# A Mamba-2, MLP and mixture-of-experts layer on one core: first transposes in two banks, statistics pinned behind a VectorE step, the output norm's chain ranked ahead, and the first MLP started a piece later

## The chip, the cores and the metric

The kernel runs on one core of a Trainium2 chip. The metric is the time on the device in microseconds (us) of one execution. Several executions are taken and their median is given. One further execution is recorded by the hardware profiler; the profile is of that one.

## The reference

The input is a sequence of 2048 tokens with 512 features, all in float32. The layer has two parts, each with a residual. The first part is a layer norm followed by an RMS norm, a Mamba-2 block, and an MLP with a gate. The second part is a layer norm and a mixture of experts with eight experts of which two are chosen for a token.

```
x = x + attn_part(layernorm(x))
x = x + moe(layernorm(x))

attn_part(v):  h = v + mamba2(rmsnorm(v, ln1_w));  h2 = rmsnorm(h, ln2_w)
               return h + silu(h2 @ gate_w) * (h2 @ up_w) @ down_w

mamba2(u):     z, xb, B, C, dt = split(u @ in_proj_w)
               xb, B, C = silu(causal_conv4(xb, B, C));  dt = softplus(dt + dt_bias)
               y = ssd_chunked(xb * dt, dt * A, B, C)        # chunks of 128 tokens, a state carried
               y = rmsnorm((y + D * xb) * silu(z), norm_w)
               return y @ out_proj_w
```

The state-space step works on chunks of 128 tokens: inside a chunk it is a masked product, and between chunks a state of 16 heads is carried on.

## The kernel before

**Tiling.** The 2048 tokens are 16 tiles of 128 tokens (index `t`) and 8 blocks of 256 tokens (index `b`, two tiles each, `j` = 0 or 1). The features lie on the partitions in four pieces of 128 (`NK` = 4). The MLP works on blocks of 512 tokens (index `fb`, four of them), which is two Mamba blocks.

**A block of the Mamba part.** `prepare(b)` (L201) takes the row statistics of the block's two tiles (`scales`, L182: bn_stats and bn_aggr on VectorE, a square root on ScalarE, a reciprocal), makes the normalised rows `hn` (L211), and turns each into columns with four TensorE transposes and one weighted copy from PSUM by VectorE (`transposed`, L189, its copy at L197). The result is `hT`. It then makes the step sizes: the product `pdt` (L228), softplus by arithmetic and an exponential, `dA` (L259), the cumulated sum `pc` (L262), and small products (L272 to L288). The rows go to memory (L267, L268) and are read back spread over the partitions by `spread` (L291: two loads of `cum` at L298 with a mask on GpSimd, and four loads of `ec` at L310 for every tile but the first). `project` (L332) makes one pair of projection columns in PSUM (`pm`, L326, weights `wi`), copies them (L338), runs the convolution on VectorE (L345, L347) and silu on ScalarE (L353). There are six such pairs, and four `gate` pairs (L355, product `pz`).

**A chunk.** `chunk(b, j, ...)` (L381) is a generator whose steps are interleaved by hand with the above. For each half of the heads (`gp`) it makes scores `psc` (L400), exponentials on ScalarE (L406), their products on VectorE (L408), for the first half the weighted inputs `xd` (L414, one buffer that is shared with `sq`), then the products `py` (L423 from the state, L431 inside the chunk) and the state's update (L438 to L459). Then the squares of y are taken on ScalarE and added on GpSimd (`sq`, L467 to L470; the last addition is kept as `summed`), the output projection `po` (L475) and the sum of squares `pms` (L478) run, and the output norm follows (L480 to L492): root and reciprocal `ry`, the new rows `h` (L484), their addition to the residual on GpSimd, a store from ScalarE's queue, a second square and root, and the scaling of `h`. The last step of a chunk turns `h` into `h2T` (L498). It is left over and run in the next chunk as `ninth`.

**PSUM.** `ps_tr` has one bank, "tr", which all transposes and the small products share. `ps_mm` has two banks, "mm", also called kind "d". `ps_y` has one bank, for `py` and `po`.

**Order of the work.** The Tile planner orders each engine's instructions by walking a model of the time: at each moment it issues the ready instruction that was traced first. Loads without an open dependency, such as those of the MLP's weights, are issued long ahead of where they are written. `tc.high_priority(n)` ranks an instruction as if traced n instructions earlier. `tc.issue_after(ins)` puts those instructions of a block that run on the engine of `ins` behind `ins` in that engine's queue; it does not make them wait for its end. From block 2 on (`BPF` = 2) TensorE's order is no longer planned: `manual_schedule` (L887) keeps it as traced. The tracing order is made by `mamba(b)` (L810), which yields 32 times in a block, and by the loop at L881, which at such a yield runs `advance()`: one piece (a quarter of one of 16 column steps) of the MLP of the 512 tokens that are done. The MLP's weights come in as `mg` (L513 to L515) and `ms` (L526); in the first MLP GpSimd makes sums and differences of them (L516, L517, L527, L528), which ScalarE's queue stores for the later ones (L529, L530).

The condition for `advance()` in the code before is

```
            if b > BPF or b == BPF and n > 1:
                advance()
```

After the last block the remaining pieces run, and after two of them the last `ninth`. The last MLP then overlaps the routing, and the experts follow.

Of the kernel before, what the change touches and what calls it, by code (L numbers as in the profile page):

```python
# [15 lines left out]
P = 128  # L16
# [33 lines left out]
def mamba_mlp_moe(ctx, tc, x, w_in, w_out, w_gu, w_down, par, wr, wg, wu, wd, out):  # L50
# [93 lines left out]
        nc.vector.bn_stats(out=st, in_=src)  # L144
        nc.vector.bn_aggr(out=dst, in_=st)

    AT_ONCE = 400

    early = const.tile([P, 1], F32, name="early")
    nc.scalar.activation(early, eps, AF.Sqrt)  # L150
# [22 lines left out]
        pool, tag = use[kind]  # L173
        return pool.tile([P, *shape], F32, name=name, tag=tag)

    idle = ps_y.tile([P, P], F32, name="idle", tag="y")
    for _ in range(20):
        nc.tensor.transpose(idle, ident, ident)

# [6 lines left out]
        nc.scalar.activation(rboth[:, lo:hi], mv[:, lo:hi, 1], AF.Sqrt, bias=eps2, scale=1.0 + EPS)  # L186
        nc.vector.reciprocal(rboth[:, lo:hi], rboth[:, lo:hi])

    def transposed(src, dst, weight=None):  # L189

        pt = bank("tr", [NK, P], "pt")
        for k in range(NK):
            nc.tensor.transpose(pt[:, k, :], src[:, k * P : (k + 1) * P], ident)  # L193
        if weight is None:
            nc.scalar.copy(dst, pt)  # L195
        else:
            nc.vector.tensor_tensor(dst, pt, bc(weight, 2, P), ALU.mult)  # L197

    first_rows = None

    def prepare(b):  # L201

        nonlocal first_rows
        hT = wa.tile([P, NK, TB], F32, name=f"hT{b}", tag="hT")
        hns = []
        with tc.issue_after(first_rows) if b == 1 else ExitStack():
            scales(b)
            for j in range(NCH):
                t = b * NCH + j
                hns.append(wa.tile([P, D], F32, name=f"hn{t}", tag="tok", bufs=3))  # L210
                normed = nc.vector.tensor_scalar(  # L211
                    hns[j], res[t], mv[:, t, 0:1], rboth[:, t : t + 1], ALU.subtract, ALU.mult
                )
        if b == 0:
            first_rows = normed.ins
        for j in range(NCH):
            yield
            transposed(hns[j], hT[:, :, j * P : (j + 1) * P], params[:, C_L1 : C_L1 + NK])

        yield hT  # L220
        lo, hi = b * NCH, (b + 1) * NCH
# [158 lines left out]

    def chunk(b, j, dt, ncum, dtdec, cd, cum, ec, xb, cs, zs):  # L381

        nonlocal summed
# [7 lines left out]
        for gp in range(2):  # L391

            if t:
                with tc.issue_after(summed):
                    nc.gpsimd.tensor_tensor(ec[:, gp], ec[:, gp], cs[gp][:, :, tok], ALU.mult)

            psc = ps_sg.tile([P, 2, 4, P], F32, name=f"psc{t}_{gp}", tag="sg")
            for half in range(2):
                rows = halves[half]
                nc.tensor.matmul(psc[:, half], xb[rows, 2 + gp, tok], cs[gp][rows, :, tok], start=True, stop=True)  # L400


            lt = cum[gp].rearrange("p (a i) q -> p a i q", a=2)
            turns = [(half, i, 8 * gp + 4 * half + i) for i in range(4) for half in range(2)]
            for half, i, h in turns:
                nc.scalar.activation(lt[:, half, i], lt[:, half, i], AF.Exp, bias=ncum[:, j, h : h + 1])  # L406
            for half, i, h in turns:
                nc.vector.scalar_tensor_tensor(  # L408
                    lt[:, half, i], lt[:, half, i], dt[:, j, h : h + 1], psc[:, half, i], ALU.mult, ALU.mult
                )  # L410
            if gp == 0 and t < NT - 1:

                xd = wa.tile([P, 4, 4, HD], F32, name=f"xd{t}", tag="xd", bufs=1)
                nc.vector.tensor_tensor(  # L414
                    xd, bc(xbt[:, 0], 2, 4),
                    bc(dtdec[:, j, :].rearrange("p (g i) -> p g i", g=4), 3, HD), ALU.mult,
                )
            if gp:
                yield
            py = ps_y.tile([P, 4, P], F32, name=f"py{t}_{gp}", tag="y")  # L420
            if t:
                for i in range(4):
                    nc.tensor.matmul(  # L423
                        py[:, i, :], sdt[:, gp, i, :], ec[:, gp, i, :], start=(i == 0), stop=False,
                        skip_group_check=True,
                    )
# [53 lines left out]
        ry = wa.tile([P, 1], F32, name=f"ry{t}", tag="ry")  # L480
        rsqrt_eps(ry, pms, scale=1.0 / DI)
        h = wa.tile([P, D], F32, name=f"h{t}", tag="tok", bufs=3)
        nc.vector.tensor_scalar(h, res[t], mv[:, t, 0:1], rstd[:, t : t + 1], ALU.subtract, ALU.mult)
        nc.vector.scalar_tensor_tensor(h, po, ry, h, ALU.mult, ALU.add)  # L484
        nc.gpsimd.tensor_tensor(res[t], res[t], h, ALU.add)
        nc.scalar.dma_start(out=resd[t], in_=res[t])

        m2 = wa.tile([P, 1], F32, name=f"m2{t}", tag="m2")
        nc.scalar.activation(sq[:, 4:8, :].rearrange("p a q -> p (a q)"), h, AF.Square, accum_out=m2)
        r2 = wa.tile([P, 1], F32, name=f"r2{t}", tag="r2")  # L490
        rsqrt_eps(r2, m2, scale=1.0 / D)
        nc.vector.tensor_scalar_mul(h, h, r2)  # L492
        yield
        fb, off = divmod(t * P, FB)
        if off == 0:
# [314 lines left out]
    def mamba(b):  # L810
# [12 lines left out]
        for j in range(NCH):  # L823
            pieces = chunk(b, j, dt, ncum, dtdec, cd, *near[j], xb, cs, zs)
            for _ in range(4):
# [55 lines left out]
    for b in range(NB):  # L881
# [296 lines left out]
```

## Time and profile before

| what | value |
|---|---|
| median of 3 runs | 1582.25 us (1581.88 to 1583.77) |
| profiled execution, its own time | 1582.87 us |
| its span, first to last instruction | 1580.9 us |
| TensorE's mean granted clock | 0.990 |
| busy: TensorE, VectorE, ScalarE, GpSimd | 1537.3, 776.9, 753.2, 404.2 us |
| memory moved | 218.68 MB, mean 138 GB/s |

In a profile PE is TensorE's matmuls, PEld its weight loads, DVE VectorE, ACT ScalarE, POOL GpSimd and SP the engine that issues most loads. A line of the timeline has the start in us, the time until the group's end in us, the engine, the line of the kernel, the operation, output and inputs with their shapes, the number of instructions, and in brackets the idle time ahead of it with what ended that. A float32 matmul appears as two records. A line of the stretches has the stretch, its length, the busy time with the number of instructions that began in it, then the granted clock, the share of the memory engines and GB/s.

### The profile page before, as it was taken

The numbers are of one execution on the slowest core, as the hardware profiler recorded it, in microseconds if no ns is written. First come the engines' busy times: TensorE is split into PE (matmuls) and PEld (weight loads), VectorE is DVE, ScalarE is ACT, GpSimd is POOL, SyncE is SP. The second block draws the span as 40 slices with busy tenths as digits, with TensorE's granted clock in tenths as the row PEclk, the third lists the DMA queues.
The fourth block names the chain that finished last, engine by engine and source line by source line (L and its number), as shares of the span: only waits on it lengthen the run. The fifth ranks groups of instructions, "written<-read, shape, count | busy, mean of one in ns | idle before, by whom it ended". The sixth has DMA issues, their size and how long they took to land. (4 is left out here: it accounts for less than half of the span.)

```text
span 1580.9 us, 19196 instructions
## 1 busy us (share of the span) xinstructions
PE 1537.3 (97%) x6303; PEld 1052.7 (67%) x6303; DVE 776.9 (49%) x2018; ACT 753.2 (48%) x1346; POOL 404.2 (26%) x510
## 2 busy tenths in 40 slices
PE   7899979999999999999999999999999999999997
PEld 6666666767666677767676777666777666555553
DVE  6776755754556464646555554434454352222221
ACT  3888796745663778457748543222211221111110
POOL 3442324333341212121212112011111123333331
PEclk8999989999999999999999999999999999999999
DMA  8443435544554553333344533238777233333332
GB/s 287 143 154 115 140 117 177 181 151 153 177 198 142 167 164 116 128 127 129 128 163 151 167 95 101 89 95 298 239 239 237 83 62 60 63 64 67 67 67 33
DMA packets 127456, 218.68 MB, mean 138 GB/s; under 512 B 11584, under 2 KB 71488, under 8 KB 127360
## 3 DMA queue, kind: packets, MB, share of 16 engines
q1 hardware_dynamic: 105088, 166.08, 33.1%
q0 software_dynamic: 8736, 20.45, 7.3%
q10 hardware_dynamic: 13536, 30.94, 5.1%
q8 instruction: 52, 0.85, 0.2%
q14 instruction: 44, 0.36, 0.1%
HBM read 176.01 MB, written 41.42 MB: 138 GB/s over the span
## 5 line engine op out<-in xcount | busy, mean ns | idle before, releaser
L685 PE MATMUL pd<-md,a 128*128 128x512 f32 x512 | 238.4, 592 | 0.0
L326 PE MATMUL pm<-hT,wi 128*128 128x256 f32 x768 | 188.9, 392 | 2.3 <-DMA wi<-in_w_in 2.3
L326 PEld LDWEIGHTS pm<-hT,wi 128*128 128x128 f32 x768 | 144.6, 195 | 27.9 <-issue 6.9
L686 DVE TENSOR_TENSOR r<-r,pd 128x512 f32<-128x512 f32 x128 | 87.6, 684 | 139.7 <-PE pd L685 139.0
L685 PEld LDWEIGHTS pd<-md,a 128*128 128x128 f32 x512 | 97.0, 190 | 74.1 <-issue 66.2
L347 DVE SCALAR_TENSOR_TENSOR ca<-pre,params,ca 128x256 f32<-128x256 f32 x288 | 135.0, 528 | 0.2
L701 PE MATMUL py<-h2T,ms 128*128 128x256 f32 x512 | 131.6, 379 | 1.6 <-POOL ms L527 0.8
L326 PE MATMUL pz<-hT,wi 128*128 128x256 f32 x512 | 118.9, 385 | 0.0
L1034 PE MATMUL epg<-ew,xgT 128*128 x312 | 118.1, 460 | 0.4 <-issue 0.2
L766 POOL TENSOR_TENSOR a<-a,up 128x256 f32<-128x256 f32 x64 | 47.3, 739 | 277.5 <-DVE up L760 240.4
L1034 PE MATMUL epu<-ew,xgT 128*128 x312 | 117.8, 459 | 0.0
L475 PE MATMUL po<-w_o,zs 128*128 128x512 f32 x256 | 112.8, 594 | 0.0
L406 ACT ACT_TABLE_LOAD x76 | 97.5, 1283 | 27.7 <-DVE ncum L274 19.2
L1055 PE MATMUL epd<-ew,ehT 128*128 (+1 forms) x234 | 107.1, 593 | 1.0 <-DVE ehT L1048 1.0
L701 PEld LDWEIGHTS py<-h2T,ms 128*128 128x128 f32 x512 | 95.6, 190 | 17.3 <-ACT up L740 1.6
L326 PEld LDWEIGHTS pz<-hT,wi 128*128 128x128 f32 x512 | 96.1, 193 | 15.6 <-issue 1.9
L406 ACT ACTIVATE cum<-cum,ncum 128x128 f32<-128x128 f32 x256 | 86.3, 393 | 7.9 <-POOL cum L300 4.3
L475 PEld LDWEIGHTS po<-w_o,zs 128*128 128x128 f32 x256 | 48.2, 190 | 57.0 <-issue 55.7
L1015 POOL DMA_INDIRECT xg<-xnd,idx x39 | 38.9, 997 | 175.9 <-PE pt L193 173.8
L1034 PEld LDWEIGHTS epu<-ew,xgT 128*128 128x128 f32 x312 | 59.3, 190 | 33.0
L1061 POOL DMA_INDIRECT out<-ey,idx x39 | 61.9, 1588 | 66.8 <-DVE ey L1060 40.8
L195 ACT COPY xgT<-pt 128x512 f32<-128x512 f32 x39 | 22.8, 587 | 117.7 <-PE pt L193 117.7
(248 smaller groups left out, 2567.7 us busy)
## 6 DMA issues: line engine op xcount, KB each, us to landing
wi<-in_w_in SPq DMA_DIRECT2D x80, 512.0 KB, 3.8
ms<-late SPq DMA_DIRECT2D x48, 512.0 KB, 3.6
mg<-early SPq DMA_DIRECT2D x48, 384.0 KB, 3.7
md<-in_w_down SPq DMA_DIRECT2D x64, 256.0 KB, 3.8
cum<-rowsd SPq DMA_DIRECT2D x32, 512.0 KB, 4.0
late<-ms ACTq DMA_DIRECT2D x16, 512.0 KB, 2.7
ec<-rowsd SPq DMA_DIRECT2D x60, 128.0 KB, 3.7
xnd<-xn ACTq DMA_DIRECT2D x28, 256.0 KB, 3.8
```

The source lines that it names most:

```text
L326: nc.tensor.matmul(pm[:, m, :], w[:, k, m * P : (m + 1) * P], hT[:, k, :], start=(k == 0), stop=(k == NK - 1))
L347: nc.vector.scalar_tensor_tensor(ca, pre[:, m, k : k + TB], cw[:, k : k + 1], ca, ALU.mult, ALU.add)
L406: nc.scalar.activation(lt[:, half, i], lt[:, half, i], AF.Exp, bias=ncum[:, j, h : h + 1])
L475: nc.tensor.matmul(po, y[:, m, :], w_o[:, m, :], start=(m == 0), stop=(m == 7))
L685: nc.tensor.matmul(pd, a[:, j * P : (j + 1) * P], d, start=(m == 0), stop=(m == 1))
L686: nc.vector.tensor_tensor(rows[j], rows[j], pd, ALU.add)
L701: nc.tensor.matmul(ps, w[:, k], m[:, k], start=(first and k == 0), stop=(k == KH - 1), skip_group_check=True)
L766: nc.gpsimd.tensor_tensor(a[:, 1], a[:, 1], up, ALU.mult)
L1015: nc.gpsimd.indirect_dma_start(out=xg, out_offset=None, in_=src, in_offset=bass.IndirectOffsetOnAxis(ap=idx[:, n : n + 1], axis=0))
L1034: nc.tensor.matmul(ps, xT[:, k, :], w[:, lo : lo + EI], start=(k == 0), stop=(k == NK - 1))
L1055: nc.tensor.matmul(pd, hT[:n, m, :], w[:n, NG + m * D : NG + (m + 1) * D], start=(m == 0), stop=(m == len(ET) - 1))
L1061: nc.gpsimd.indirect_dma_start(out=out, out_offset=bass.IndirectOffsetOnAxis(ap=idx[:, n : n + 1], axis=0), in_=y, in_offset=None, compute ...
```

## The change

1. `transposed` takes the kind of bank. In `prepare(0)` the second tile's transposes use a bank of kind "d" instead of "tr". Five more idle transposes follow them (`idling(5)`).
2. The statistics and normalised rows of every block but the first are put behind a VectorE instruction: those of block 1 behind the copy of block 0's last transposes, those of a later block b+1 behind `xd` of tile 2b. Before, only block 1 was held, behind block 0's last `hn`.
3. The output norm (L480 to L492) is traced under `tc.high_priority(100)`.
4. The GpSimd sums of the first MLP's early weights are put behind the newest `summed`.
5. In the first stage `spread` of tile 1 is traced after all six pairs instead of after the third.
6. In `mamba` the leftover `ninth` comes one yield later, after the step of `halves` instead of ahead of it, and the first MLP's first piece one yield later (`n > 2`).

```diff
-    AT_ONCE = 400
+    AT_ONCE, SOON = 400, 100
...
-    idle = ps_y.tile([P, P], F32, name="idle", tag="y")
-    for _ in range(20):
-        nc.tensor.transpose(idle, ident, ident)
+    def idling(n):
+        idle = ps_y.tile([P, P], F32, name="idle", tag="y")
+        for _ in range(n):
+            nc.tensor.transpose(idle, ident, ident)
+
+    idling(20)
...
-    def transposed(src, dst, weight=None):
-
-        pt = bank("tr", [NK, P], "pt")
+    def transposed(src, dst, weight=None, kind="tr"):
+
+        pt = bank(kind, [NK, P], "pt")
...
-            nc.vector.tensor_tensor(dst, pt, bc(weight, 2, P), ALU.mult)
-
-    first_rows = None
+            return nc.vector.tensor_tensor(dst, pt, bc(weight, 2, P), ALU.mult).ins
+
+    behind = None
...
-        with tc.issue_after(first_rows) if b == 1 else ExitStack():
+        with tc.issue_after(behind) if b else ExitStack():
             scales(b)
...
-        if b == 0:
-            first_rows = normed.ins
         for j in range(NCH):
             yield
-            transposed(hns[j], hT[:, :, j * P : (j + 1) * P], params[:, C_L1 : C_L1 + NK])
+            kind = "d" if b == 0 and j else "tr"
+            turned = transposed(hns[j], hT[:, :, j * P : (j + 1) * P], params[:, C_L1 : C_L1 + NK], kind)
+            if b == 0:
+                behind = turned
+                if j:
+                    idling(5)
...
-                nc.vector.tensor_tensor(
+                added = nc.vector.tensor_tensor(
                     xd, bc(xbt[:, 0], 2, 4),
...
+                if t:
+                    behind = added.ins
...
+        with tc.high_priority(SOON):
+            ry = wa.tile([P, 1], F32, name=f"ry{t}", tag="ry")
+            rsqrt_eps(ry, pms, scale=1.0 / DI)
...
+            nc.vector.tensor_scalar_mul(h, h, r2)
         yield
...
-            nc.gpsimd.tensor_tensor(w[:, 1], w[:, 3], w[:, 1], ALU.add)
-            nc.gpsimd.tensor_tensor(w[:, 2], w[:, 1], w[:, 0], ALU.subtract)
+            with tc.issue_after(summed):
+                nc.gpsimd.tensor_tensor(w[:, 1], w[:, 3], w[:, 1], ALU.add)
+                nc.gpsimd.tensor_tensor(w[:, 2], w[:, 1], w[:, 0], ALU.subtract)
...
-            near = [spread(0, j, ready[-1]) for j in range(NCH)]
+            near = [spread(0, 0, ready[-1])]
             nc.sync.dma_start(out=w_o, in_=w_out.rearrange("(t p) n -> p t n", p=P))
+    near.append(spread(0, 1, ready[-1]))
...
                 next(pieces)
+                next(halves, None)
+                yield
                 if n % 4 == 0:
                     finish(ninth)
-                next(halves, None)
-                yield
...
-            if b > BPF or b == BPF and n > 1:
+            if b > BPF or b == BPF and n > 2:
                 advance()
```

More of the change, by code (lines that the diff above doesn't have):

```diff
@@ L196, in transposed @@
         else:
-            nc.vector.tensor_tensor(dst, pt, bc(weight, 2, P), ALU.mult)
-    first_rows = None
+            return nc.vector.tensor_tensor(dst, pt, bc(weight, 2, P), ALU.mult).ins
+    behind = None
     def prepare(b):
-        nonlocal first_rows
+        nonlocal behind
         hT = wa.tile([P, NK, TB], F32, name=f"hT{b}", tag="hT")
         hns = []
-        with tc.issue_after(first_rows) if b == 1 else ExitStack():
+        with tc.issue_after(behind) if b else ExitStack():
             scales(b)
@@ L210, in prepare @@
                 hns.append(wa.tile([P, D], F32, name=f"hn{t}", tag="tok", bufs=3))
-                normed = nc.vector.tensor_scalar(
+                nc.vector.tensor_scalar(
                     hns[j], res[t], mv[:, t, 0:1], rboth[:, t : t + 1], ALU.subtract, ALU.mult
                 )
-        if b == 0:
-            first_rows = normed.ins
         for j in range(NCH):
             yield
-            transposed(hns[j], hT[:, :, j * P : (j + 1) * P], params[:, C_L1 : C_L1 + NK])
+            kind = "d" if b == 0 and j else "tr"
[4 more added lines that the diff above has]
+                    idling(5)
         yield hT
@@ L381, in chunk @@
     def chunk(b, j, dt, ncum, dtdec, cd, cum, ec, xb, cs, zs):
-        nonlocal summed
+        nonlocal summed, behind
         t = b * NCH + j
@@ L478, in chunk @@
         nc.tensor.matmul(pms, sq[:, 0, :], ones[:, 0:1], start=True, stop=True)
[L480 to L492, printed above, removed]
+        with tc.high_priority(SOON):
+            ry = wa.tile([P, 1], F32, name=f"ry{t}", tag="ry")
+            rsqrt_eps(ry, pms, scale=1.0 / DI)
+            h = wa.tile([P, D], F32, name=f"h{t}", tag="tok", bufs=3)
+            nc.vector.tensor_scalar(h, res[t], mv[:, t, 0:1], rstd[:, t : t + 1], ALU.subtract, ALU.mult)
+            nc.vector.scalar_tensor_tensor(h, po, ry, h, ALU.mult, ALU.add)
+            nc.gpsimd.tensor_tensor(res[t], res[t], h, ALU.add)
+            nc.scalar.dma_start(out=resd[t], in_=res[t])
+            m2 = wa.tile([P, 1], F32, name=f"m2{t}", tag="m2")
+            nc.scalar.activation(sq[:, 4:8, :].rearrange("p a q -> p (a q)"), h, AF.Square, accum_out=m2)
+            r2 = wa.tile([P, 1], F32, name=f"r2{t}", tag="r2")
+            rsqrt_eps(r2, m2, scale=1.0 / D)
+            nc.vector.tensor_scalar_mul(h, h, r2)
         yield
```

## The prediction

> **What bounds the kernel now.** I read the page's busy table and slices first, then TensorE's own waits, then the clock by stretches, then the timeline of the places that these named.
>
> ```profile
> PE 1537.3 (97%) x6303; PEld 1052.7 (67%) x6303; DVE 776.9 (49%) x2018; ACT 753.2 (48%) x1346; POOL 404.2 (26%) x510
> ...
> PE   7899979999999999999999999999999999999997
> ```
>
> TensorE (PE) is busy for 97% of the span. Only 1580.9 - 1537.3 = 43.6 us are idle, and the slices under 9 lie in the first 240 us and at the end. From 300 to 1500 us the stretches add to about 5.4 us of idle. A change that takes no matmul away can therefore win only in the first 240 us. TensorE's waits, longest first (total, times, longest):
>
> ```profile
> PE pt L193 <- DVE mv L145: 7.1, 1, 7.1
> PE py L423 <- POOL halo L340: 4.0, 2, 2.4
> PE pc L262 <- POOL pre L339: 3.4, 1, 3.4
> PE pm L326 <- DMA wi<-in_w_in: 2.3, 1, 2.3
> PE pt L193 <- DVE hT L197: 1.9, 1, 1.9
> ```
>
> The releaser is the last by semaphore, not always the cause. The POOL copies at L339 and L340 take 0.2 us and gate nothing here: pc waits for dA (L259, done at 27.81 us), and py waits for h (L484) to empty the one bank of ps_y.
>
> Idle time also slows what follows. Stretches, with TensorE's busy time, then its granted clock:
>
> ```profile
> 27.00:29.10 2.10, 1.15 (x6) 1.00 1.03 399
> 29.10:32.50 3.40, 3.40 (x10) 0.50 0.71 211
> 32.50:36.00 3.50, 3.50 (x20) 0.99 0.91 233
> ...
> 46.10:49.50 3.40, 3.40 (x10) 0.51 0.55 202
> ...
> 203.20:213.50 10.30, 4.47 (x13) 0.50 0.22 70
> ```
>
> [...] The timeline has the places:
>
> ```profile
> 8.88 1.12 PE L193 MATMUL pt<-ident,hn 128*128 128x128 f32 x4 [1.87 <-DVE hT L197]
> 10.78 3.60 PE L228 MATMUL pdt<-w_dt,hT 128*128 128x16 f32 x16 [0.78 <-DVE hT L197]
> 14.21 10.32 PE L326 MATMUL pm<-hT,wi 128*128 128x256 f32 x36
> 20.28 0.69 DVE L144 BATCH_NORM_STATS2 bn<-x 128x6 f32<-128x512 f32 x1 [3.46 <-DMA x<-in_x]
> 27.95 0.38 PE L262 MATMUL pc<-tri,dA 128*32 128x128 f32 x2 [3.42 <-POOL pre L339]
> 45.49 5.41 PE L326 MATMUL pm<-hT,wi 128*128 128x256 f32 x16 [2.35 <-DMA wi<-in_w_in]
> 206.63 1.21 DVE L414 TENSOR_TENSOR xd<-xbt,dtdec 128x1024 f32<-128x1024 f32 x1
> 209.03 1.08 PE L193 MATMUL pt<-ident,h 128*128 128x128 f32 x4 [7.07 <-DVE mv L145]
> 209.91 5.37 PE L326 MATMUL pz<-hT,wi 128*128 128x256 f32 x16
> ```
>
> The DVE line shows the statistics of tile 4, which belong to block 2, in the middle of block 0's softplus: VectorE stands 3.46 us for a load that nobody needs yet, and dA comes late.
>
> [...]
>
> **Part by part.**
>
> *Start, 6 to 61 us.* The second transposes go to a "mm" bank, so the 1.87 us wait goes. The statistics of blocks 1 and 2 leave the front of VectorE, so hT is copied at about 7.1 and 7.8 us instead of 8.15 and 10.03, and the 0.78 us before pdt goes too. pdt would run from 7.9 us. With few gaps the clock should hold. Matmuls at full clock: 16 pdt take 1.85 us (67.22 us) and 16 pm take 3.62 us (74.06 us), so half clock cost 1.75 us on pdt, 10.32 - 36 x 0.226 = 2.2 us on pm, and 0.5 us on pt. dA comes without the 3.46 us stall: the 3.42 us wait and about 1.6 us of slow clock after it go. The broadcast loads of chunk 1 (L298, L310) no longer stand before wi of pair 5 on SP's queue; they stood there until 40.25 us, waiting for rowsd. The 2.35 us wait and 1.8 us of slow clock go. TensorE's side sums to 1.87 + 0.78 + 0.5 + 1.75 + 2.2 + 3.42 + 1.6 + 2.35 + 1.8 = 16.3 us.
>
> Two things come late next. The loads: wi of pairs 0 and 1 landed a median 7.1 us after issue, so at about 10.7 us, 0.8 us after pdt; wi of pair 3 is issued at 14.5 us or later and stands behind w_o (landed 19.6 us), x and the MLP's ms (22.1 us), at 400 GB/s, so it lands at 22 to 23.5 us, against 21.7 us when three pairs are done. I charge 2 us: 14 us are left. Then VectorE: a pair's convolution is 2 x (0.31 + 3 x 0.48) = 3.5 us, six pairs 21 us, and the first starts after pm 0, at 15.0 instead of 20.98 us: 6.0 us. About 3.5 us of its later idle was waiting for TensorE (0.44 at 30.43 us, 1.15 at 29.80, 2 of the 3.0 before 52.01) and goes. So py at 61.17 us can move by about 9.5 us, and TensorE's other 4.5 us turn into a wait for VectorE there, as the four gates (14.5 us) do not cover more. ScalarE did 34.7 us up to 63 us and also allows it; its 4.41 us idle before 25.25 us, behind the ACT-queue writes of the MLP's weights, goes since those now come at 195 us. I take **-9.5**; bounds -3 (loads late, ScalarE full) and -15.
>
> *Five idle transposes*: 5 x 0.15 = 0.8 us at most, beside a wait for hn of 0.63 us: **+0.2** (0 to +0.5).
>
> *Output norm in front* (L480 to L492). Its rank moves ahead of the 100 instructions traced before it. What delayed ry at 123 and 199 us and r at 206.43 us on ScalarE was mostly exp and silu traced after it, taken since ready; rank does not change that. The waits of py are 2.4 and 1.5 us. **-0.5** (0 to -3).
>
> *Block 2's beginning, 202 to 219 us.* Before, TensorE stood 7.07 us for h, then ran 0.5 + 1.75 us slow. Now one gate (16 pz, 3.62 us) comes ahead of the transposes, from 202 to 205.6 us, and the MLP starts a piece later. But the next item in TensorE's fixed order is the transposes of hn, and hn's statistics now queue on VectorE behind xd, which ended at 207.84 us. From there: 2 x 0.67 + 2 x 0.17 = 1.7 us, a table load and root on ScalarE 1.28 + 0.29 with up to 1 us of queue, reciprocal 0.15, hn 0.54: 212 to 213 us. Then pt 0.6, gate 3.62 with up to 1.75 of slow clock, pt 0.6: the MLP's first product at 217.3 to 219.4 us, against 219.01 + 0.6 with the same work done. **-1.2** (+2 to -8, the last if xd and the statistics come ahead of the convolution).
>
> *The same order in blocks 1 to 6.* The transposes of h (L498) and of hn (L218) now stand back to back in the one bank "tr"; a gate lay between them before. The second set waits for the copy of the first: 0.69 us at L197 (347.93 + 0.60, copy 348.57 to 349.26). In block 2 this lies under the wait for hn, in block 1 the planner can part them. Blocks 3 to 6: 4 x 0.8 = **+3.2**. Bounds: the copy began 0.03 to 0.2 us after the transposes at these places, but up to 2.9 us after at others (98.70 us). In these blocks hn itself is in time: xd ended at 339.2 us, the transposes ran at 354.41 us, 15 us later against a chain of 5.
>
> *POOL's sums of the first MLP's weights* (L516, L517), each 0.8 to 0.9 us, go from 21 to 27 us to after sums of chunk 3 at 194.7 us. Behind them stand POOL's ec, state and a. POOL is idle 196 to 200 and 202 to 208 us: **0**. Cover gone, each costs its 0.9 us; one wait of this kind is there now (0.80 us at 255.16 us).
>
> *The last piece* of the MLP after the last block: moved, not added. 0.
>
> Sum: -9.5 + 0.2 - 0.5 - 1.2 + 3.2 = **-7.8 us**. The profiled execution took 1582.87 us, 2.0 more than its span and 0.6 over the median of 1582.25. Against the median: **1574.5 us**.
>
> **Rivals.** *Gate cover works whole*: hn is ready by 207 us, so block 2 gains 8 us instead of 1.2, and the start gains 11 or 12: 1582.3 - (11.5 + 0.5 + 8 - 3.2 - 0.2) = 1565.7 us. For it: TensorE asks only 3.62 + 0.6 + 0.8 us of cover. Against: xd waits for the square of h (202.57 us) and stood behind the convolution and L408. *The start is taken by loads and ScalarE*: the memory engines moved 400 GB/s from 10 to 19 us, ScalarE is 89% busy from 60 to 80 us; the start gains 3: 1581 us. Against: the MLP's 1.3 MB of early writes leave this stretch. *Slower: the copy in bank "tr" is late*. Place: L197 between L498 and L218 in blocks 2 to 6. Price 5 x (delay + 0.75). It outweighs the 11 us of gains from a delay of 1.5 us on; at 2.9 us it is 18.3 us: 1589.5 us. For it: such delays are in the trace where VectorE was in a convolution. Against: at these places it answered within 0.2 us.
>
> **How the numbers follow.** Within 0.2% (3.2 us) a measurement cannot tell from no change. The forecast, 1569 to 1579 us, 0.50; whole cover 0.20; start taken 0.19; slower 0.11. The start-taken case is split 0.10, 0.07, 0.02 over faster, the same and slower. Faster 0.50 + 0.20 + 0.10 = 0.80, same 0.07, slower 0.02 + 0.11 = 0.13. The range leaves out the worst of the slower case and the far end of the best one: 1561.5 to 1582.5 us.
>
> **What would show it.** Right: pt at 7 to 8 us without a wait, no statistics with a DMA wait on VectorE, pc and pair 5's pm without waits, py of chunk 0 at about 51.5 us; a new wait of pt for h2T (L197) of about 0.8 us in four or five blocks; hn's wait at block 2. Wrong: long new TensorE waits at 25 to 60 us for wi or silu; L197 copies over 1 us late; TensorE waiting for POOL's sums in the first MLP.

## The result and the profile after

The changed kernel takes 1597.16 us (median of 6 runs, 1594.77 to 1598.65) against 1582.9 us (median of 6 runs of the kernel before beside it, 1580.96 to 1584.23). The ratio is 1.0088, with a 95% interval of 1.0075 to 1.0101: it is **slower by 0.9%**, 14.3 us. The forecast was 7.8 us faster, and its range ended at 1582.5 us. The profiled execution took 1597.42 us, its span is 1595.7 us, and TensorE's mean granted clock 0.989.

The first view is the page's busy table and slices of the changed kernel.

```profile
PE 1543.7 (97%) x6308; PEld 1051.4 (66%) x6308; DVE 770.5 (48%) x2018; ACT 741.4 (46%) x1335; POOL 399.9 (25%) x510
...
PE   9999888999999999999999999999999999999997
```

The early slices are fuller than before: the start did gain. The idle time is 1595.7 - 1543.7 = 52.0 us, 8.4 more than before, and busy time rose by 6.4 us with five instructions more. From the first product of the MLP to the experts TensorE is idle for 21.0 us, against 5.6 before, in waits that are too short to show in slices of 40 us; ahead of that stretch it is idle for 7 us less than before. TensorE's own waits show them (total, times, longest, in us):

```profile
PE px L711 <- DVE a L775: 9.9, 7, 1.8
PE py L431 <- POOL halo L346: 7.5, 2, 5.0
PE pt L196 <- DVE hn L214: 4.8, 2, 3.7
PE pt L196 <- DVE h2T L200: 3.1, 4, 0.8
```

(Lines have moved: transposes are L196, their copy L200, the MLP's product L711, the weight stores L539 and L540.) The first line was forecast nowhere: the MLP's products wait for their own bank (0.5 us, once, before the change). The fourth is the one that the forecast named, 4 x 0.78 us.

**Where the time went.** I marked the start of each tile's output projection (`po`, L483; L475 before), of the first MLP product (`px`), and of the experts in both traces. Changed minus before:

| mark | after - before, us |
|---|---|
| `po` of tile 0 | -9.95 |
| `po` of tile 3 | -9.0 |
| first `px` (MLP starts) | -4.4 |
| `po` of tile 4 | -4.3 |
| `po` of tile 6 | +2.1 |
| `po` of tile 8 | +4.3 |
| `po` of tile 12 | +9.7 |
| experts start | +14.8 |

Marks with a sign are such differences below too; before the change `po` of tile 0 starts at 78.93 us. So there are two stories. The start gains 10 us, as forecast (9.5). Then 4.6 us go at block 2's beginning, between `po` of tile 3 and the first `px`, and 19.2 us while MLP pieces and blocks share the engines. The experts add nothing.

**Block 2's beginning.** The timeline of the changed kernel, GpSimd, ScalarE with its queue (ACTq), and TensorE:

```profile
189.99 1.40 POOL L527 TENSOR_TENSOR mg<-mg 128x256 f32<-128x256 f32 x2
190.74 0.33 ACTq L539 DMA_DIRECT2D early<-mg  x1
192.10 0.33 ACTq L540 DMA_DIRECT2D late<-ms  x1
192.45 1.28 ACT L139 ACT_TABLE_LOAD   x1 [3.16 <-POOL pre L345]
195.21 2.05 PE L431 MATMUL py<-ec,sdiag 128*128 128x128 f32 x8 [4.98 <-POOL halo L346]
203.27 0.63 PE L196 MATMUL pt<-ident,h 128*128 128x128 f32 x4 [1.51 <-DVE mv L145]
207.63 1.09 PE L196 MATMUL pt<-ident,hn 128*128 128x128 f32 x4 [3.73 <-DVE hn L214]
```

Read from the top: the pinned sums run on GpSimd until 191.4 us and the difference made of them (L538) until 192.1; ScalarE's queue holds the two stores of these, and only behind them stands the table load for `ry`. ScalarE stood 3.16 us. The releaser that the line names, a copy at L345, gates nothing; e3 below shows that it is the sums. So `ry`, `h` and with it `py`'s bank come late: `py` waits 4.98 us (1.53 before). The wait of `pt` for h fell from 7.07 to 1.51 us, but one for hn of 3.73 us follows. The clock was 0.50 from 192.4 to 199.2 and from 206.1 to 212.9 us, 13.6 us in all against 10.2 us before.

**The border of two column steps.** The next view is the timeline at one of the seven places where `px` waits:

```profile
267.51 1.88 PE L695 MATMUL pd<-md,a 128*128 128x512 f32 x4
267.70 0.29 ACT L139 ACTIVATE r<-m,singles 128x1 f32<-128x1 f32 x1
268.01 1.28 ACT L739 ACT_TABLE_LOAD   x1
269.30 0.42 ACT L739 ACTIVATE a<-a 128x256 f32<-128x256 f32 x1
269.43 0.69 DVE L696 TENSOR_TENSOR r<-r,pd 128x512 f32<-128x512 f32 x1 [1.72 <-PE pd L695]
270.30 0.49 DVE L501 TENSOR_SCALAR h<-h,r 128x512 f32<-128x512 f32 x1
270.70 0.41 DVE L775 TENSOR_TENSOR a<-a,px 128x256 f32<-128x256 f32 x1
271.17 1.13 PE L711 MATMUL px<-h2T,mg 128*128 128x256 f32 x4 [1.78 <-DVE a L775]
```

The last product of a column is in `px`'s one bank. VectorE's multiplication (L775) empties it, and for that it needs the silu (L739), which stands on ScalarE behind the output norm's root (L139) and a table load. The silu ends at 269.72 us; on VectorE the multiplication then still stands behind an addition (L696) and the output norm's scaling (L501). TensorE's next matmul is the first product of the next column, into the same bank. It waits 1.78 us. Four of the seven waits look like this, 6.9 us in all; in the other three (0.51, 1.70 and 0.79 us) nothing of the norm stands right ahead.

### The profile page after: what moved, and what is told of

The parts are those of the page before. It is cut to its first block, busy times and chain, and to the rows that moved or that the text cites. A ratio compares the mean times of both kernels' runs of the same rounds, so it can differ in the third digit from the quotient of the medians.

```text
span 1595.7 us, 19155 instructions
## 1 busy us (share of the span) xinstructions
PE 1543.7 (97%) x6308; PEld 1051.4 (66%) x6308; DVE 770.5 (48%) x2018; ACT 741.4 (46%) x1335; POOL 399.9 (25%) x510
## 5 line engine op out<-in xcount | busy, mean ns | idle before, releaser
L332 PE MATMUL pm<-hT,wi 128*128 128x256 f32 x768 | 183.3, 384 | 1.3 <-DVE r L696 0.9
L696 DVE TENSOR_TENSOR r<-r,pd 128x512 f32<-128x512 f32 x128 | 87.6, 684 | 149.1 <-PE pd L695 148.0
L332 PEld LDWEIGHTS pm<-hT,wi 128*128 128x128 f32 x768 | 140.7, 190 | 26.2 <-issue 8.8
L353 DVE SCALAR_TENSOR_TENSOR ca<-pre,params,ca 128x256 f32<-128x256 f32 x288 | 141.2, 543 | 0.3
L711 PE MATMUL py<-h2T,ms 128*128 128x256 f32 x512 | 132.1, 380 | 0.9 <-ACT up L750 0.7
L332 PE MATMUL pz<-hT,wi 128*128 128x256 f32 x512 | 123.3, 394 | 0.6 <-DMA wi<-in_w_in 0.6
L483 PE MATMUL po<-w_o,zs 128*128 128x512 f32 x256 | 112.9, 592 | 0.0
L711 PEld LDWEIGHTS py<-h2T,ms 128*128 128x128 f32 x512 | 95.0, 190 | 18.0 <-DVE a L744 2.4
L412 ACT ACTIVATE cum<-cum,ncum 128x128 f32<-128x128 f32 x256 | 87.1, 394 | 14.7 <-POOL cum L306 12.3
L483 PEld LDWEIGHTS po<-w_o,zs 128*128 128x128 f32 x256 | 48.3, 190 | 55.5 <-issue 54.0
L711 PE MATMUL px<-h2T,mg 128*128 128x256 f32 x256 | 68.0, 388 | 10.7 <-DVE a L775 9.9
```

What stands on the lines that cost most here:

```text
L332: nc.tensor.matmul(pm[:, m, :], w[:, k, m * P : (m + 1) * P], hT[:, k, :], start=(k == 0), stop=(k == NK - 1))
L353: nc.vector.scalar_tensor_tensor(ca, pre[:, m, k : k + TB], cw[:, k : k + 1], ca, ALU.mult, ALU.add)
L483: nc.tensor.matmul(po, y[:, m, :], w_o[:, m, :], start=(m == 0), stop=(m == 7))
L696: nc.vector.tensor_tensor(rows[j], rows[j], pd, ALU.add)
L711: nc.tensor.matmul(ps, w[:, k], m[:, k], start=(first and k == 0), stop=(k == KH - 1), skip_group_check=True)
```

## The experiments

Each ratio is to the kernel before, run beside it (medians 1582.2 to 1582.8 us). My theory after the trace: the MLP's later piece costs some 12 to 15 us, the pinned sums 4 to 5, the order of the two sets of transposes 4, and the start's parts give 10. The main rival: the piece is innocent, and the norm's chain in front or the pins slow every block.

### The MLP's piece

**e1_piece_earlier**: the changed kernel with the old condition.

```diff
-            if b > BPF or b == BPF and n > 2:
+            if b > BPF or b == BPF and n > 1:
```

> The changed kernel with the first MLP's first piece at the yield where it was before (n > 1); everything else of the change stays. Theory: the later start put the border between two column steps of the MLP at the one yield of four that carries no Mamba work, so the next step's first product asks for the bank px only 0 to 1.9 us after the last one wrote it, and also shifted the pieces that stood between two users of the bank tr. Then the px waits for a (9.9 us in the changed kernel) go, and with them the pc waits for xbt and the late tr waits of the routing: 11 to 15 us less, 1582 to 1586 us. Rival (the norm's chain put in front makes silu and so a late): the px waits stay, 1595 us or more.

Measured 1582.41 us, ratio 0.9997 (0.9987 to 1.0006): 14.8 us of the 1597.2 are gone with this digit. The wait of `px` for L775, 9.9 us in seven places, is left with this line:

```profile
PE px L711 <- DVE a L775: 0.5, 1, 0.5
```

**e4_piece_later_alone**: the kernel before with `n > 2` and nothing else.

> The kernel before with one edit: the first MLP's first piece one yield later (n > 2). Theory of the shifted pieces: 8 to 15 us slower than before, 1591 to 1598 us, with px waits for a of 7 to 12 us. Rival (the loss needs the other parts of the change): within 3 us of before.

Measured 1593.56 us, 1.0074 (1.0057 to 1.0091): 10.8 us lost by the digit alone, with `pc` waiting 2.5 us for the copy of `xbt`, and `px` less than the 7 to 12 us of the theory:

```profile
PE px L701 <- DVE a L765: 4.1, 3, 2.6
```

That the digit costs this time is shown from both sides. That most of it is the wait for `px`'s bank holds in the changed kernel alone.

**e2_norm_not_in_front**: the changed kernel without the higher rank of the output norm.

```diff
-        with tc.high_priority(SOON):
+        with ExitStack():
```

> The changed kernel without the high priority on the output norm. Theory of the shifted pieces: px waits stay at 7 to 12 us, total within 3 us of the changed kernel, 1594 to 1600 us. Rival (the norm's chain in front delays silu): px waits fall below 3 us and the time to 1588 us or less.

Measured 1590.34 us, 1.0051 (1.0034 to 1.0068), and `px` waits 6.7 us less than in the changed kernel:

```profile
PE px L711 <- DVE a L775: 3.2, 4, 1.7
```

Neither forecast was met: the rank is worth a loss of 6.8 us where the piece is late. It is the four places with the norm's chain ahead of silu and multiplication: 0.2 us of their 6.9 is left. So some 6.8 of the late piece's 14.8 us need the rank as well; that e4, which has no rank, loses 10.8 us and not 8 is not explained. With the piece where it was I did not take the rank away alone; e12 below keeps it and ends where e14, without it, ends.

**e6_other_bank_first**: the piece late, but from the second column on the product into the other bank runs first.

```diff
+            if c:
+                order[0]()
             product(x1, early[:, 0], b11)
...
-            order[0]()
+            if c == 0:
+                order[0]()
```

> The changed kernel whole, with the MLP's piece late as it has it, but in the first piece of every column step but the first, the product that goes to px's other bank (p5, into py) runs ahead of the product into px. Same work, one order changed. Theory: the late piece costs its time because px's single bank is asked for again before VectorE has multiplied the last column's out of it; about 1 us of other matmuls ahead covers that: PE's waits of px for a fall from 9.9 us to under 3, and the time from 1597.2 to 1585 to 1590 us. Rival: the bank is only where it shows, and the time lies in the engines' load beside block work (ScalarE, table loads): the waits move to py for up or to the next piece, and the time stays at 1594 us or more.

Measured 1591.82 us, 1.0063 (1.0049 to 1.0076). Its waits of `px` for a, and of `pc` for a copy on ScalarE:

```profile
PE px L711 <- DVE a L778: 3.7, 5, 0.9
...
PE pc L268 <- ACT xbt L381: 2.6, 2, 1.5
```

6.2 us of wait for the bank are gone and 5.4 us of time: the bank is a cause, and not the whole. Neither forecast was met here either: `px` was to wait under 3 us and the time to fall to 1585 to 1590 us, or to stay at 1594 or more. Of the 9.4 us that still part this kernel from e1, TensorE's waits from the first `px` on show 6.9: 3.2 of `px`, 2.6 of `pc`, and the rest short waits of `pms`, `pm` and `ptx`, less some that e1 has and this kernel has not. No wait names the other 2.5 us.

### Block 2's beginning, and the bank of the transposes

**e3_sums_not_pinned**: the changed kernel with GpSimd's sums free.

```diff
-            with tc.issue_after(summed):
+            with ExitStack():
```

> The changed kernel with GpSimd's sums of the first MLP's weights no longer behind the sum of squares. Theory: pinned, the sums of the first two column steps run at 188 to 192 us, and the stores of them on ScalarE's queue hold ry behind them, which makes py of tile 4 wait 5.0 us instead of 1.5. Freed, that wait falls to 1 to 2.5 us and the MLP begins 3 to 5 us earlier; in exchange the stores are back at the start and may cost it 1 to 4 us: 1592 to 1597 us in all, and no change in the px waits. Rival (the pin costs nothing, ry is late for another reason): the wait of py at the beginning of block 2 stays at 5 us.

Measured 1592.42 us, 1.0072 (1.0053 to 1.0092), 4.7 us less than the change. `po` of tile 0 stays at -9.65 us, the first `px` comes at -10.1 instead of -4.4. The sums' pin gives the start nothing and costs about 5 us by the MLP's start. TensorE's waits of this kernel:

```profile
PE px L711 <- DVE a L775: 9.8, 7, 1.8
PE pt L196 <- DVE hn L214: 6.0, 2, 5.0
PE py L431 <- POOL halo L346: 4.1, 2, 3.1
```

Of the 5.7 us at the first `px`, 2.4 lie in block 2's beginning: no store stands ahead of `ry`, `py` waits 3.14 us instead of 4.98, and the wait for hn is longer, 4.96 us. The other 3.3 us are there at `po` of tile 3 (-12.3 instead of -9.0), before a pinned sum runs: `py` waits 0.98 us at 115.72 us, instead of 2.49 at 117.36, and the clock does not fall there (0.50 from 117.3 to 120.7 us in the changed kernel). Why the pin reaches back to that place is not shown.

**e5_gate_between**: the piece where it was, and `finish(ninth)` ahead of the step of `halves` as before.

> The changed kernel with the MLP's piece where it was and with the next block's pair of channels (ninth) ahead of the output transposes again, so that a gate lies between the transposes of h and those of hn. Theory: what the two sets of transposes back to back in bank tr cost (four waits of 0.78 us, an excess of 3.8 us in all) goes, and the wait for hn at block 2 (up to 5.0 us) gets a gate as cover: 1582.4 of the kernel with the piece where it was, less 4 to 7, so 1575 to 1578.5 us, and no wait of pt for h2T in blocks 3 to 6. Rival: the copies are hidden by the work that the planner puts there, and the gate only moves the wait for h back to 7 us at block 2: 1582 us or more.

Measured 1577.18 us, 0.9975 (0.9964 to 0.9987): 5.2 us less than e1. No wait of `pt` for h2T is left; from `po` of tile 5 to that of tile 15 this kernel keeps 5.4 us to the kernel before without moving, where e1 goes from -5.1 to -0.6. The forecast's +3.2 us for this order was right, if a little small.

**e9_stats_as_before**: the piece where it was, the statistics pinned only as in the kernel before.

```diff
-        with tc.issue_after(behind) if b else ExitStack():
+        with tc.issue_after(first_rows) if b == 1 else ExitStack():
```

> The changed kernel with the MLP's piece where it was (1582.4 us), and the blocks' statistics as before: block 1's behind the first block's hn, the later ones behind nothing. Two banks, idle transposes and loads stay as changed. Theory: the pin is what carries the start's 10 us (VectorE stood 3.46 us for the statistics of a tile that is not needed yet, and its convolutions came that much later): po of tile 0 goes back by 3.5 to 8 us, to 72 to 76 us; the hn wait at block 2 (5.0 us) goes, which gives 3 to 5 back: 1582 to 1588 us. Rival: the start's gain comes from TensorE's side (two banks, clock, loads), po of tile 0 stays within 1 us of 68.3, and with the hn wait gone the time is 1577 to 1580 us.

Measured 1576.92 us, 0.9967 (0.9955 to 0.998): 5.5 us less than e1. The theory on the start fell: `po` of tile 0 is at 69.7 us without the pin. The time is just under the rival's range. The pin costs more than it gives here: with it (e1) `po` of tile 0 comes 1.4 us earlier, but the wait for hn is then 5.0 us, and 0.9 in this kernel.

### The start

**e7_no_five_idle** (the piece where it was, without the line `idling(5)`), **e8_start_one_bank** (the piece where it was, `kind = "tr"` throughout) and **e10_chunk1_early** (the piece where it was, both `spread` calls after the third pair again) each take one part of the start back.

> The changed kernel with the MLP's piece where it was (1582.4 us) and without the five idle transposes behind the second set of block 0. Theory: they cost 0.2 us and are worth more by keeping the clock full: without them the clock is 0.5 for one or two pieces of 3.4 us around 8 to 14 us, which puts pdt or pm 1.8 to 3.6 us later, and the first block's output (po of tile 0) 0 to 3 us later, since VectorE sets the pace there: 1582.5 to 1585 us. Rival: [...] the idle ones are only cost: 1581.5 to 1582.3 us with the clock at 1.00 up to 20 us.

e7 measured 1584.93 us, 1.0011 (1.0 to 1.0022), 2.5 us over e1; the stretch of 10 to 20 us has a clock of 0.83 instead of 1.00, and `po` of tile 1 comes 2.6 us later. The clock doesn't settle the cause: e9 has the five transposes, and 0.83 as well.

> The changed kernel with the MLP's piece where it was (1582.4 us) and with both sets of block 0's transposes in bank tr again. Theory (the sum's term of 1.87 us for the bank, with 6 us in all for VectorE's earlier first convolution): the second set waits about 1 us for the first copy, hT comes about 1 us later, and everything up to po of tile 0 moves by that: 1583 to 1584.5 us. Rival: the bank is the main part of the start's 10 us, because the gap also lets the clock fall: po of tile 0 3 us or more later and 1585.5 us or more. Second rival: it is hidden behind loads: 1582.4 us, no change.

e8 measured 1583.87 us, 1.0006 (0.9999 to 1.0013), and `po` of tile 0 is at -10.3 us: nothing is lost there.

> The changed kernel with the MLP's piece where it was (1582.4 us), with chunk 1's broadcast loads ahead of w_o and of the next pairs' wi on SP's queue as before. Theory: the 2.35 us wait of pm for wi (pair 5) and some 1.8 us of slow clock come back, but VectorE's convolutions set the start's pace, so po of tile 0 moves by less than 1.5 us: 1582 to 1584.5 us. Rival: the loads are the start's bottleneck, po of tile 0 goes back by 3 us or more and the time to 1585.5 us or more.

e10 measured 1582.87 us, 1.0001 (0.9992 to 1.0009), `po` of tile 0 at -11.2 us. The wait for wi is 2.5 us again, and nothing comes of it.

So each of four parts, and the sums' pin with e3, can go without the start losing its 10 us. Either two parts do the same thing, or I had not found the thing.

**e13_stats_and_loads** takes two parts back together (edits of e9 and e10).

> The changed kernel with the MLP's piece where it was, with both the blocks' statistics and chunk 1's loads as before. Each of these alone left the start's gain (po of tile 0 at 69.7 and 67.7 us, 78.9 before). Theory: they cover each other, either keeps VectorE from standing for the load of a tile that is needed later; with both taken back the wait of 3.46 us comes again, VectorE's first convolution starts at 19 us or later and po of tile 0 is at 72 to 78 us: 1580 to 1586 us against 1576.9 with the statistics alone. Rival: the two banks and idle transposes do it, po of tile 0 stays below 71 us: 1576 to 1578 us.

Measured 1578.78 us, 0.9973 (0.9964 to 0.9982). The theory fell: VectorE's first convolution began at 16.92 us and nothing stood for the load. `po` of tile 0 is at 71.9 us and the time at 1578.8, both between the two forecasts.

So the question was turned round: one part alone in the kernel before. **e14_banks_alone** has the two banks and the five idle transposes, **e15_stats_pin_alone** the pin of the statistics.

> The kernel before with the two banks and the five idle transposes alone. Theory: VectorE's stop for the early tile at 20 us sets the first convolution, so the matmuls come earlier but po of tile 0 moves by less than 2.5 us from 78.9: 1579.5 to 1582.5 us. Rival: TensorE's side is the start's limit, po of tile 0 moves by 7 us or more: 1572 to 1576 us.

e14 measured 1571.32 us, 0.9928 (0.9913 to 0.9944). The theory fell: `po` of tile 0 is at -10.1 us, as the rival had it, and the experts at -12.2; the time is 0.7 us below the rival's range.

> The kernel before with the pin of the blocks' statistics alone. Theory: VectorE's first convolution starts at 16 to 18 us instead of 20.98, po of tile 0 is at 71 to 75 us; at block 2's start the wait for hn replaces the 7.07 us wait, 0 to 4 us lost: 1576 to 1581 us. Rival: the pin does nothing for the start (po of tile 0 within 1.5 us of 78.9), since convolution waits for a slow TensorE: 1582 to 1586 us.

e15 measured 1579.9 us, 0.9978 (0.9967 to 0.999), `po` of tile 0 at 76.2 us, less gain than expected, with a new 6.4 us wait for wi.

**e17_bank_alone** has nothing but the other bank, **e18_idle_alone** nothing but the idle transposes.

```diff
-    def transposed(src, dst, weight=None):
-        pt = bank("tr", [NK, P], "pt")
+    def transposed(src, dst, weight=None, kind="tr"):
+        pt = bank(kind, [NK, P], "pt")
...
+            kind = "d" if b == 0 and j else "tr"
```

> The kernel before with block 0's second set of transposes in another bank, without the five idle ones. Theory: the 1.87 us wait goes, pm 0 runs some 2 to 3 us earlier (12 us), at half clock for one piece at most, and that is enough for VectorE to have its convolution before it reaches the statistics of the early tile: po of tile 0 at 69 to 72 us, 1572 to 1575.5 us. Rival: without the idle transposes the gaps at 8 to 11 us halve the clock for both pdt and pm as before, po of tile 0 at 74 us or later: 1577 us or more.

e17 measured 1572.62 us, 0.9935 (0.9917 to 0.9954): **the bank alone is enough**, 10.2 us, as its theory had it. Its timeline:

```profile
6.48 1.11 PE L193 MATMUL pt<-ident,hn 128*128 128x128 f32 x8 [1.06 <-DVE hn L211]
9.00 1.96 PE L229 MATMUL pdt<-w_dt,hT 128*128 128x16 f32 x16 [1.41 <-DVE hT L197]
10.81 9.70 PE L327 MATMUL pm<-hT,wi 128*128 128x256 f32 x36
16.93 0.36 DVE L346 TENSOR_SCALAR ca<-pre,params 128x256 f32<-128x256 f32 x1 [3.04 <-ACT pre L339]
20.68 0.68 DVE L144 BATCH_NORM_STATS2 bn<-x 128x6 f32<-128x512 f32 x1
```

> The kernel before with the five idle transposes behind block 0's second set, which stays in bank tr. Theory: the 1.87 us wait stays, and with it the clock falls before the idle ones come; pdt may run full after them, pm 0 1 to 2 us earlier, po of tile 0 at 75 to 79 us: 1578 to 1582.5 us. Rival: it is the clock that counts, not the bank: pdt and pm at full clock, po of tile 0 at 72 us or less, 1575.5 us or less.

e18 measured 1583.64 us, 1.0003 (0.9994 to 1.0012): no gain, with `po` of tile 0 where the theory had it (77.7 us) and the time 1.1 us above its range. Its timeline has the difference:

```profile
19.32 0.69 DVE L144 BATCH_NORM_STATS2 bn<-x 128x6 f32<-128x512 f32 x1 [4.16 <-DMA x<-in_x]
20.02 0.35 DVE L350 TENSOR_SCALAR ca<-pre,params 128x256 f32<-128x256 f32 x1
```

In e18, as before the change, the statistics of tile 4 stand ahead of the first convolution in VectorE's order, and VectorE stood 4.16 us for their load. In e17 the same statistics stand 16 places further back, behind the first convolution and the rest of the softplus. They run at 20.68 us with no wait: the load has landed meanwhile. An earlier TensorE is not what e18 lacks: its `pm` starts at 12.57 us, 1.6 us before the old place, and 36 of them take 9.70 us as in e17, yet `dA` comes at 26.59 us, against 20.55 in e17. Why the planner turned the two is only argued: with the bank's wait gone the convolution is ready, in its model of the time, before VectorE is free for the statistics. The bank takes 1.87 us off TensorE's path, and with it an order on VectorE turns over that is worth more.

The traces also say how each part could go without loss: two parts do the same thing. VectorE's wait for that load (2.5 to 4.2 us) is in just the three kernels that have neither the other bank nor the pin: the one before, e4 and e18. With the bank and without the pin it is at most 0.5 us (e9, e13, e14, e16, e17), and with the pin and without the bank there is none (e8, e15). e8 keeps the whole gain at `po` of tile 0 without the bank. The pin alone keeps 2.7 us: `dA` comes at 23.44 us instead of 27.63, but `pdt` still takes 3.60 us, and at 44 us TensorE stands 6.4 us for wi.

### The sums

**e11_best_of_parts**: e5, and the sums of GpSimd free.

> The changed kernel with three of its parts taken back together: the MLP's piece where it was, a gate between the two sets of transposes, POOL's first sums not pinned. Theory: the three costs are separate and add: 1577.2 of the first two, less the 3.5 to 5 us that the pinned sums cost at block 2's start: 1572 to 1574 us, with py's longest wait at about 3 us and not 5. Rival: with the gate between, the 5 us wait of py is followed by another (h or hn at 200 to 212 us) that is fixed by VectorE, so freeing the sums gives under 1.5 us: 1576 to 1577.5 us.

Measured 1572.07 us, 0.9934 (0.9921 to 0.9948). The time is in the theory's range: the free sums give 5.1 us here, on e5, and gave 4.7 on the changed kernel (e3), so this cost hardly depends on the other two. The longest wait of `py` is 3.1 us. Another did follow, though, for h:

```profile
PE pt L196 <- DVE h L501: 5.4, 2, 4.8
PE py L431 <- POOL halo L346: 4.5, 2, 3.1
```

**e12_best_one_pin**: e11 with the later blocks' statistics pinned once, behind `xd` of tile 1 (`if t == 1`). **e16_best_no_pin**: e11 with the statistics pinned as before the change.

> As the kernel with the three parts taken back, and the statistics of blocks 2 and later pinned once, behind xd of tile 1, and not behind the newest xd each time. Theory: the last wait of pt for hn at block 2's start (3.2 us) goes, since the statistics are done long before; 2 to 3.5 us less than that kernel: 1569 to 1571.5 us. Rival: the freed statistics only move ahead of VectorE's convolution and delay it by their 1.7 us, and the wait is then for h: no gain, 1572 to 1574 us.

Measured 1571.0 us, 0.9928 (0.9915 to 0.9942). The wait for hn is gone, but the gain on e11 is 1.1 us, inside the intervals.

> The best kernel (MLP's piece where it was, a gate between, sums free; 1572.1 us) without the pin of the blocks' statistics. Theory: the pin's cost is only the wait for hn at block 2, which the kernel with one pin (1571.0 us) had already lost; the start keeps its gain: 1569.5 to 1572 us. Rival: the statistics then stand in front of VectorE's early work and the start loses what e3 kept: 1574 us or more.

Measured 1574.12 us, 0.9945 (0.9928 to 0.9961). The median lies where the rival had it, but `po` of tile 0 is at -10.05 us, so the start lost nothing, and the interval covers e11 and e12: not settled, and small. The best versions are e12 (1571.0), e14 (1571.3), e11 (1572.1) and e17 (1572.6), which these runs don't part. The last has one new argument and beats both kernels, by 10 us and 24.5 us.

## Why the prediction was wrong, step by step

**"The last piece of the MLP ... moved, not added. 0."** This is the step that failed. The matmuls were indeed the same. But the piece that is moved sets where each column step of the MLP begins among the yields of the block. Measured, the digit costs 10.8 us in the kernel before and 14.8 in the changed one. Part of it is `px`'s bank, which the next column asks for right after the last one: from e1 to the changed kernel its wait grows by 9.4 us, and putting another bank's product first wins 5.4 us (e6). The rest is in part short waits for other banks and copies, and in part named by no wait. I looked only at what the moved piece does at the end, and not at every border that it shifts.

**"Output norm in front: -0.5 (0 to -3)."** Where the piece is late the sign was wrong, and the bound: 6.8 us of loss (e2). I priced whom the rank helps, and not the silu that it is put ahead of on ScalarE, where the norm's root took a table load of 1.28 us (at 266.40 us) and silu a second one of 1.28 us (at 268.01 us), nor the multiplication behind the norm's scaling on VectorE.

**"POOL is idle 196 to 200 and 202 to 208 us: 0" for the sums.** Measured 4.7 and 5.1 us of loss (e3, e11). The sums found room on GpSimd. But their stores are issued from ScalarE's queue, and there they now stand ahead of the output norm: 3.16 us of an idle ScalarE, just as VectorE stood 3.46 us in the kernel before. I had counted these stores as a gain where they leave (4.41 us of ScalarE ahead of 25.25 us) and not as a cost at 195 us, where I wrote that they go. The stores belong to the 2.4 us at block 2's beginning; the 3.3 us ahead of it stay unexplained.

**"Block 2's beginning -1.2 (+2 to -8)."** Measured +4.6 as a whole, and +2.1 with the sums free (e3). The wait for hn came, as forecast (3.73 us), but hn came later than forecast: at 207.6 us, which is 216.6 us when the start's 9.0 us are put back, against "212 to 213". What the pin costs can't be added to that: without it 5.5 us are won where the sums are pinned and no gate lies between (e9), and about nothing where the sums are free and the gate is back (e16). That the waits lie one behind the other at the same place would explain it; no run shows which of the two differences counts.

**"+3.2" for the back-to-back transposes.** The place and the wait were right: four waits of 0.78 us, in the blocks named. By e5, which also puts a gate ahead of hn at block 2, the order is worth 5.2 us. The copies were not late: the rival that ended slower had its place right and its delay wrong, and the loss came from elsewhere.

**"Start -9.5."** The size was right, -9.95 at `po` of tile 0, but in part by luck. `py` of chunk 0, put at about 51.5 us, ran at 45.31 us, behind a wait of 2.12 us for VectorE, as forecast in kind. Then TensorE worked from 45.7 to 55.8 us without a gap at a clock of 0.50, which no term has; by my estimate from these 10.1 us that took back some 5 us. And the sum had four parts, while one is enough (e17): the statistics leave the front of VectorE by the pin, as I wrote, or by the bank, where I saw only the 1.87 us on TensorE. To write another bank than the one being read was worth more here than the wait it takes away: 1.87 us of wait gone, 10.2 us won (e17).

**"Five idle transposes +0.2."** With them 1.3 us less (e14 against e17, inside the intervals), 2.5 us less (e1 against e7, at their edge), and nothing won by them alone (e18): if anything a small gain, and not shown to come through the clock.

**The rivals.** Neither of the two better or neutral cases came, as the start was won and block 2 lost. The chance of 0.13 on slower rested on late copies and on a start that loads take, neither of which the runs show; the border of the column steps was in no case.

In sum, by the chain of kernels from the changed one over e1 and e5 to e11: the piece 14.8 us against 0 in the forecast, the order of the transposes with block 2's beginning 5.2 against +3.2 - 1.2 = 2.0, the sums 5.1 against 0, and what e11 keeps -10.2 against -9.5 + 0.2 - 0.5 = -9.8. A chain adds up by its making (14.9, with 14.3 measured directly), so this is no test of the parts; it says where the 22 us between forecast and result lie, two thirds of them in the piece.

## What to carry to other kernels

A yield or a due time that is moved by one shifts every later meeting of two interleaved streams; ask which single bank is asked for right after it was filled, at each border, before calling it free (here `px`'s, 9.9 us of waits). Price a delayed step on every queue that its instructions and its stores pass, with what stands behind them there (here 3.16 us of an idle ScalarE behind two stores). And when several edits aim at one place, try each one alone in the old kernel: here one new argument was enough for the whole gain, a second part did the same thing over again, and three others cost 25 us.

## What was not expected of the hardware

At the start the clock stayed at 1.00 up to 20 us in the changed kernel and in e14, and 36 `pm` took 8.02 us; in e7 and e17, without the five idle transposes, it was 0.83 from 10 to 20 us, and they took 9.70 us. That looks like the work of the idle transposes. But e9 and e13 have them, and there too the clock was 0.83 and the 36 `pm` took 9.70 us. Yet e14 and e17 end within 1.3 us, with `po` of tile 0 only 1.0 us apart.

Nor do these traces say what makes the clock fall. In the kernel before it was 0.50 behind three stretches of 3.4 us with 1.05 to 1.15 us busy (25.7 to 29.1, 42.7 to 46.1 and 199.8 to 203.2 us), and stayed at 1.00 behind 39.3 to 42.7 us with 1.67 us. But it stayed at 1.00 as well from 126.0 to 129.5 us, behind 122.6 to 126.0 us with 0.96 us busy and a wait of `py` of 2.44 us. What decides it stays open.

In the changed kernel the 20 idle transposes at the very start follow each other every 0.21 us up to 4.56 us and every 0.11 us from 4.73 us, with no other matmul ahead of 6.49 us. The clock record of that run begins at 4.68 us, with 1.00; what ended the slower pace is not shown.
